# Softmax sums of a four-layer graph network on one core: layer 2's weights folded onto half the partitions and summed in one step of row and column tiles, layer 1's chunks summed on VectorE, biases added in pieces

## The chip, the cores and the metric

The kernel runs on one core of a Trainium2 chip. The core has a matrix engine (TensorE, PE in the profile, with its weight loads listed as PEld), three engines for elementwise work (VectorE is DVE, ScalarE is ACT, GpSimd is POOL), a queue engine (SyncE, SP) and 16 DMA engines. SBUF is the on-chip memory of 128 partitions; PSUM is where TensorE writes. Each engine works through its own instructions in order, and semaphores tie them together. The metric is the device time of one execution in microseconds. Before the change it was 2972.38 us, the median of 3 runs (2971.67 to 2974.36).

## The reference

32 graphs, each with 512 nodes of 256 features and a dense 512x512 adjacency matrix, go through four layers. Every layer adds its result to its input and normalises over the features.

```python
x = layernorm(x + gin(x, adj, eps, W1, b1, W2, b2))         # relu((1+eps)x + adj x) W1 ..., W2
x = layernorm(x + gat(x, adj, W, a_src, a_dst, bias))       # 4 heads, masked by adj > 0.5
x = layernorm(x + attention(x, adj, Wq, Wk, Wv, Wo, bo))    # 8 heads, scores + log(adj + 1e-6)
x = layernorm(x + masked_attention(x, nodemask, adj, W))    # 1 head, scores * adj
```

The code calls these layers 0 to 3. In layers 1 and 2 the attention weights of a head are exponentials e[j, i] of source node j and target node i. The output for target i is the sum over j of e[j, i] v[j], divided by the sum over j of e[j, i]. The change is about these divisors. All data are float32.

## The kernel before, in words

Weights of a head lie with the source nodes on the partitions: 512 sources are four chunks of 128 partitions, and each chunk has 512 targets along the free axis. So a divisor is a sum over chunks and over partitions, and TensorE makes the sum over partitions with a matrix of ones.

The work of each graph is cut into named steps. A step names an engine, an estimated time, the steps that it comes after, and the buffers that it takes and frees. Class `Plan` (line 47) walks over the steps of all graphs, with up to six graphs open at a time, and writes out the order of the instructions on every engine. It goes by due times and by a table of shifts per step name, which stands with a few other numbers in the last call, `plan.run`. The emitted order is then fixed: each engine does its instructions in that order and waits where data are late. Steps of graph g+1 and g+2 are thus mixed with those of graph g. Buffers come from counted stocks: 11 of 8 KB per partition ("B"), 12 of 4 KB ("C"), 17 of 2 KB ("D") and 8 PSUM banks ("p"). Step names carry numbers: h is a head, c a chunk, o a half of layer 2's heads, k = 4o + c.

The parts that the change and the prediction touch are these.

* Biases (`bias_steps`, L584): POOL adds one of three bias rows to the graph's x, 128 partitions by 1024 elements, in one instruction. x has to be ready before the layer's residual sum. These are the steps xb1, xb2 and xb3.
* Layer norm (`norm_steps`): VectorE takes statistics (L587, L588), adds epsilon to the variance (L604, on four elements), POOL raises it to the power -0.5 (L610, the rstd steps), VectorE makes a shift (L618), and ScalarE applies both (L628).
* Layer 0: transposes of the adjacency (L682), adj x (L715), the two products (L738, L757).
* Layer 1: ScalarE and VectorE make the weights of head h in buffer e{h}, four chunks of 512 (L909, L920; VectorE's steps are zm). The steps o1 (L943) multiply weights by values, two heads side by side as column tiles of 64, for chunks 0 and 1 and then for chunks 2 and 3. Steps ad{h}0 and ad{h}1 (L971) let an accumulating DMA, issued by POOL, add chunks 2 and 3 to chunks 0 and 1, and then chunk 1 to chunk 0. Step d1 (L991) sums the remaining chunk over partitions in column tiles of 32. The names aq and as that follow a DMA hold no instruction; they stand for its time on the queue and until landing.
* Layer 2: steps s{k} (L1113) make scores of chunk c for four heads at once, as four row tiles of 32; ScalarE takes exponentials (L1126, steps e), and VectorE multiplies with the adjacency (L1135, steps m, two heads each) into the buffer E{k} of 128 partitions by 4 heads by 512 targets. Steps n{k} (L1171) multiply weights by values, four heads side by side as column tiles of 32. Accumulating DMAs issued by POOL (`collect`, L1146, steps cd) add chunk 1 to chunk 0, chunk 3 to chunk 2, and then chunk 2 to chunk 0. One step d20 and one step d21 per graph (L1201) sum over the partitions: four column tiles of 32, each with a 128x32 matrix of ones, for four heads. ScalarE copies the result (L1213), VectorE takes the reciprocal (L1220, two halves) and multiplies (L1225), and the output projection follows (L1256). In the last graph no DMA collects the chunks, and d2 runs over all four chunks of each half.
* Layer 3: projections (L1300), scores (L1314), row maxima and exponentials, transposes (L1353), the product with x (L1368).

Of the kernel before, what the change touches and what calls it, by code (L numbers as in the profile page):

```python
# [14 lines left out]
ALU = mybir.AluOpType  # L15
AX = mybir.AxisListType

P = 128
# [209 lines left out]
def fast_path(  # L228
# [23 lines left out]
    nc = tc.nc  # L252
    B, N, D = x.shape
# [303 lines left out]
    def graph(g):  # L557
# [20 lines left out]
        def bias_steps(k, after):  # L578


            @step(f"xb{k}", "pool", 2.5, after + ("^bias",))
            def _():
                b = bias_bc[:, k - 1, None, :].to_broadcast([P, NC, D])
                nc.gpsimd.tensor_tensor(t["x"], t["x"], b, ALU.add)  # L584

        def norm_stats(n, c):
            nc.vector.bn_stats(t[f"st{n}"][:, c, :], t["xo" if n == 4 else "x"][:, c, :])  # L587
# [372 lines left out]
        plan.free("v1", ("o101", "o111"))  # L960

        for h in range(H1):
            after = (f"o1{h//2}0", f"zm{h}1")
            for k, m in enumerate((2, 1)):

                @step(f"ad{h}{k}", "pool", 0.95, after)
                def _(h=h, m=m):
                    z = t[f"e{h}"].rearrange("p c n -> p (c n)")  # L970
                    nc.gpsimd.dma_start(  # L971
                        z[:, : m * N], z[:, m * N : 2 * m * N], accum_op=ALU.add
                    )

                @step(f"aq{h}{k}", "qa", 1.5 * m, (f"ad{h}{k}",))
                def _():
                    pass

                @step(f"as{h}{k}", None, 2.5, (f"aq{h}{k}",))
                def _():  # L980
                    pass

                after = (f"as{h}{k}",)


        @step("d1", "pe", 0.95, tuple(f"as{h}1" for h in range(H1)), take=("p=d1",), mode="c32")
# [172 lines left out]
        def attend(k):  # L1159
# [26 lines left out]
                nc.scalar.copy(t["yT2"][:, o, :], t[f"n{o}"])  # L1186

            a = NC * o
            chunks = range(a, a + NC) if last else (a,)
            if not last:  # L1190
                collect(a + 2, a, (f"cs{a+1}", f"cs{a+3}", f"n{a+2}"))

            @step(
                f"d2{o}", "pe", 0.855 * len(chunks),
                tuple(f"m{b}1" for b in chunks) if last else (f"cs{a+2}",), take=(f"p=d2{o}",), mode="c32",
            )
            def _():
                t[f"d{o}"] = bank(f"d2{o}", [P, N], f"d2_ps_{o}")
                for b in chunks:
                    for j in range(4):  # L1200
                        nc.tensor.matmul(  # L1201
                            t[f"d{o}"][32 * j : 32 * j + 32, :], ones[:, :32], t[f"E{b}"][:, j, :],
                            start=(b == a), stop=(b == chunks[-1]),
                        )

            for b in chunks:
                for key in (f"E{b}", f"zs{b}"):
                    plan.free(key, (f"d2{o}", f"n{b}"))

            @step(f"nd{o}", "act", 0.49, (f"d2{o}",), take=(f"D=rdT{o}/1",), free=(f"d2{o}",))  # L1210
            def _():
                t[f"rd{o}"] = strip(f"rdT{o}", [P, N], f"rdT_{o}")
                nc.scalar.copy(t[f"rd{o}"], t[f"d{o}"])  # L1213
# [199 lines left out]
    for g in range(B):  # L1413
        graph(g)
    with tc.manual_schedule():
        plan.run([(28, 0.0, 6, 55.0, ((824592, 5.0), (893565, 10.0), (244737, 10.0), (23294, 5.0), (814168, 2.0), (264532, 2.0), (583369, 2.0), (708249, 5.0), (118144, 2.0), (603753, 2.0), (522046, 10.0), (973053, 5.0), (608632, 2.0), (603770, 2.0)), (0.5, 0.0, 0.0), (('Rl.q', 5.0), ('Rli', -10.5), ('Rs.q', -4.5), ('Rsi', 8.0), ('Rt', -14.5), ('ST', 4.5), ('ab', -6.0), ('ad00', -62.0), ('ad01', -61.5), ('ad10', -77.0), ('ad11', -51.5), ('ad20', -67.0), ('ad21', -32.5), ('ad30', -65.0), ('ad31', -48.0), ('aq00', 15.5), ('aq01', -16.0), ('aq10', 1.5), ('aq11', 2.5), ('aq20', -5.0), ('aq21', -5.0), ('aq30', 19.5), ('aq31', 61.0), ('at0', -1.5), ('at1', -36.0), ('at2', -12.0), ('at3', 8.5), ('atd0', 12.0), ('atd1', 5.0), ('atd2', -1.5), ('atd3', 6.5), ('ate0', 9.0), ('ate1', -57.5), ('ate2', 11.0), ('ate3', -0.5), ('cd1', -20.0), ('cd2', -16.5), ('cd3', -23.0), ('cd5', -10.0), ('cd7', -10.0), ('cq1', 6.0), ('cq2', -4.5), ('cq3', -55.5), ('cq6', -9.0), ('cq7', -15.0), ('d1', 4.5), ('d20', -2.5), ('d21', -4.5), ('de', -3.0), ('dev2.0', -11.0), ('dev4.0', -18.0), ('dt', -3.5), ('e00', -46.5), ('e02', -5.0), ('e03', 10.0), ('e10', -34.0), ('e12', -1.0), ('e13', -2.0), ('e20', -1.0), ('e21', -9.0), ('e22', -95.0), ('e23', -32.0), ('e30', -52.0), ('e31', -24.5), ('e32', -8.5), ('e33', 1.0), ('e42', -36.5), ('e43', -2.0), ('e50', -2.0), ('e51', -44.5), ('e53', -78.5), ('e60', -60.0), ('e61', -38.5), ('e62', -20.0), ('e63', -26.0), ('e70', -17.0), ('e71', -45.0), ('e72', -77.0), ('e73', -5.0), ('ed0', 46.5), ('ed1', 13.5), ('ed2', -19.5), ('ed3', 2.5), ('f0', 12.0), ('f1', 15.0), ('f3', -1.5), ('fe0', -12.0), ('fe1', -15.5), ('fe2', -8.0), ('fe3', 3.5), ('h0', -21.0), ('h1', -29.5), ('he0', -1.0), ('he1', 13.0), ('hsb.q', -1.0), ('hsbi', -2.0), ('hsl', -7.0), ('i0', 27.5), ('i1', 5.5), ('ie0', -1.0), ('ie1', 13.5), ('k0', -33.0), ('k1', 1.5), ('ke0', -10.0), ('ke1', 14.0), ('la0.q', 2.0), ('la0i', -32.0), ('la1.q', -32.5), ('la1i', -33.5), ('la2.q', -8.0), ('la2i', 20.0), ('la3.q', -3.0), ('la3i', 2.0), ('lb0.q', -44.0), ('lb0i', -35.0), ('lb1.q', 5.0), ('lb1i', -5.0), ('lb2.q', -33.0), ('lb2i', -37.0), ('lb3.q', -27.0), ('lb3i', -15.0), ('ldn.q', 3.0), ('ldni', -12.0), ('lx.q', 10.0), ('m00', -2.0), ('m01', 23.5), ('m10', 28.0), ('m20', 18.0), ('m21', -24.5), ('m30', 24.0), ('m31', 6.5), ('m40', 1.5), ('m41', -5.5), ('m50', 18.0), ('m51', -6.5), ('m60', 13.0), ('m61', 12.0), ('m70', 2.0), ('m71', 8.0), ('n0', 3.5), ('n1', 1.0), ('n2', -8.5), ('n4', 4.5), ('n5', -18.0), ('n6', -1.5), ('n7', 6.0), ('nd0', 16.0), ('nd1', -13.0), ('no0', 15.0), ('no1', 5.5), ('node', 11.5), ('o100', -38.5), ('o101', -4.5), ('o110', 3.0), ('o111', 5.5), ('oe0', 21.5), ('oe1', 78.5), ('out0.q', 7.0), ('out0i', 12.0), ('p0', 4.0), ('p1', -0.5), ('q0', 8.0), ('q1', 2.5), ('qe1', 2.0), ('r10', 1.0), ('r11', 15.0), ('r12', 81.5), ('r13', 10.0), ('r20', -12.5), ('r21', -15.5), ('r22', -4.0), ('r30', 2.0), ('r31', 46.0), ('r33', 4.5), ('r40', 42.5), ('r42', -15.5), ('r43', 4.5), ('rc00', 21.0), ('rc01', 0.5), ('rc10', 13.5), ('rd30', -10.0), ('rd32', 3.0), ('rd33', 2.0), ('s0', -1.5), ('s1', -36.0), ('s2', -2.0), ('s3', 0.5), ('s4', 14.0), ('s5', 3.5), ('s6', 6.5), ('s7', 8.5), ('sh1.0', 4.0), ('sh2.0', -31.5), ('sh3.0', 2.0), ('sh4.0', -3.0), ('st10', -1.0), ('st11', 13.5), ('st12', 24.5), ('st20', -7.5), ('st21', -8.0), ('st22', 7.0), ('st31', -3.0), ('st32', 3.0), ('st33', -8.5), ('st40', 6.0), ('st41', -6.5), ('st42', 6.5), ('st43', 20.5), ('t0', -7.0), ('t2', -8.5), ('t3', 0.5), ('ta0', -1.0), ('ta2', -3.0), ('ta3', -8.0), ('tb0', 4.0), ('tb1', 3.5), ('tb2', -10.5), ('tb3', 20.0), ('te1', -26.0), ('te2', -21.5), ('te3', 10.0), ('u0', 0.5), ('u1', -1.0), ('u2', -8.5), ('u3', -0.5), ('ue0', 1.5), ('ue1', 2.0), ('ue3', 22.0), ('v10', 8.0), ('v12', 10.0), ('v13', -1.5), ('v20', 1.0), ('v21', 1.5), ('v22', -14.5), ('v23', -35.5), ('va1.0', -19.0), ('va3.0', -0.5), ('ve10', 30.0), ('ve11', 10.0), ('ve12', 22.0), ('ve13', 31.5), ('ve20', 117.0), ('ve21', 58.0), ('ve22', 1.0), ('ve23', 6.5), ('w0', -2.0), ('w1', 2.0), ('w2', -17.0), ('w3', 5.5), ('wx0', -2.0), ('wx1', -1.0), ('wx2', -2.0), ('wx3', -15.5), ('x10', 4.5), ('x11', -10.0), ('x30', -22.0), ('x31', -13.0), ('xb1', -45.5), ('xb3', 2.0), ('xe10', 2.0), ('xe11', -61.5), ('xe20', -20.5), ('xe21', -8.5), ('xe30', 6.5), ('xe31', 3.5), ('xs.q', -1.5), ('xsi', 9.0), ('xt10', 9.5), ('xt20', 0.5), ('xt30', -2.0), ('xt31', -9.5), ('y0', 2.0), ('y1', -5.5), ('yd00', -21.0), ('yd01', 0.5), ('yd10', 10.5), ('yd11', -12.5), ('yn0', 7.5), ('yn1', 20.0), ('yn2', 26.0), ('yn3', 6.5), ('yt1', -3.0), ('yt2', -9.5), ('yt3', 5.5), ('z00', 9.5), ('z01', 4.5), ('z02', -18.0), ('z03', 51.0), ('z10', -2.0), ('z11', 3.0), ('z12', -1.0), ('z13', 31.0), ('z20', -2.0), ('z21', -21.0), ('z22', 45.0), ('z23', -4.0), ('z30', 40.0), ('z31', 3.0), ('z32', -27.5), ('z33', 10.0), ('zm00', -52.0), ('zm01', -4.5), ('zm10', -2.0), ('zm11', 7.0), ('zm20', -19.5), ('zm21', 7.5), ('zm30', -7.5), ('zm31', 2.0)))])

# [470 lines left out]
```

## Time and profile before

| what | value |
|---|---|
| median of 3 runs | 2972.38 us |
| time of the profiled execution | 2971.27 us |
| its span (first to last instruction) | 2969.4 us |
| mean granted TensorE clock | 0.997 |
| d2 (L1201) | 560 matmul records, 72.6 us busy |
| layer 1's DMA issues (L971) | 256, 512 KB and 256 KB by turns |
| layer 2's DMA issues (L1146) | 186 of 1024 KB |
| bias steps (L584) | 96, mean 2555 ns |
| software DMA queue | 295.73 MB, 51.4% of the 16 engines' span |
| all DMA | 448.93 MB, mean 151 GB/s |

How to read it: a row of a group of instructions has the line, engine and operation, written and read tiles with their shapes, the count, busy time and mean length of one in nanoseconds, and the idle time of the engine just before them with what ended it. A form such as 128*32 ahead of a shape is the part of TensorE's array that is used (rows by columns). A float32 matmul of two distinct data operands leaves two records. TensorE's matmuls are pipelined, so its busy share says that it always has something under way, not that it runs at its peak. The chain follows the work that ended last back from the end, at each step to what released it.

### The profile page before, as it was taken

The page shows a single profiled execution, that of the slowest core. Times are in us where ns is not written, and L with a number is a line of the kernel's source. Part 1 is how long each engine was busy: PE and PEld are TensorE (multiplying, and loading weights), DVE is VectorE, ACT ScalarE, POOL GpSimd, SP SyncE. Part 2 cuts the span into 40 slices and gives each one's busy share as a digit, 9 for nine tenths or more (in the row PEclk, how much of TensorE's full clock was granted, in tenths as well). Part 3 has the DMA queues.
Part 4 walks back from the last instruction along what each step waited for, and adds up shares of the span by engine and source line. Part 5 has one row for each costly group of instructions (what it writes and reads, how often), then busy time and mean ns, then how long its engine had stood idle before and what let it go on. Part 6 is the DMA issues. An engine that isn't in the chain of part 4 may idle for free.

```text
span 2969.4 us, 42791 instructions
## 1 busy us (share of the span) xinstructions
PE 2943.3 (99%) x15521; PEld 1668.0 (56%) x15521; DVE 2150.4 (72%) x4133; ACT 1927.3 (65%) x3818; POOL 801.4 (27%) x688
## 2 busy tenths in 40 slices
PE   8999999999999999999999999999999999999998
PEld 6545555555556555555555555555655555554545
DVE  3677777777777777677676777777777767767777
ACT  4666665667666676666676666766667666667664
POOL 1323222223232322222222222323232222223220
PEclk9999999999999999999999999999999999999999
DMA  4677766677766686666776666776668666677680
GB/s 146 137 156 174 165 153 140 145 158 169 166 146 140 140 183 162 154 134 143 176 165 155 137 148 156 170 166 146 139 140 185 159 156 133 142 176 157 138 178 16
DMA packets 153368, 448.93 MB, mean 151 GB/s; under 512 B 15232, under 2 KB 55360, under 8 KB 125248
## 3 DMA queue, kind: packets, MB, share of 16 engines
q0 software_dynamic: 63648, 295.73, 51.4%
q1 hardware_dynamic: 88112, 149.75, 15.4%
q8 instruction: 125, 2.05, 0.3%
q10 hardware_dynamic: 1392, 0.66, 0.1%
q14 instruction: 91, 0.75, 0.1%
HBM read 133.30 MB, written 17.07 MB: 51 GB/s over the span
## 4 chain that ended last, share of the span: by engine, by line
PE 85%; DVE 13%; DMA 1%; ACT 0%; issue 0%; POOL 0%; POOLq 0%; SPq 0%; ACTq 0%
PE h1T_ps L738 8%; PE s L1314 8%; PE hT_ps L715 8%; PE o_ps L1368 7%; PE y_ps L757 7%; PE o_ps L1171 6%; PE s L1113 6%; PE o_ps L943 5%; DVE z L1135 4%; PE v_ps L806 4%; PE v_ps L1094 4%; PE iT_ps L1300 4%; PE kT_ps L1076 4%; PE qT_ps L1076 4%; DVE st L587 2%; PE d_ps L1201 2%
## 5 line engine op out<-in xcount | busy, mean ns | idle before, releaser
L1126 ACT ACTIVATE z<-s 128x512 f32<-128x512 f32 x1024 | 551.3, 605 | 250.2 <-PE s L1113 250.0
L1135 DVE SCALAR_TENSOR_TENSOR z<-AT,z 128x1024 f32<-128x1024 f32 x512 | 625.6, 1241 | 95.7 <-ACT z L1126 93.0
L920 DVE SCALAR_TENSOR_TENSOR z<-z,T,edge 128x512 f32<-128x512 f32 x512 | 416.8, 857 | 38.2 <-ACT z L909 38.1
L1146 POOL DMA_DIRECT2D z<-z x186 | 164.1, 884 | 1005.5 <-DMA z<-z 358.7
L909 ACT ACTIVATE z<-R_bc,nT,S 128x512 f32<-128x512 f32 x512 | 376.6, 807 | 31.6 <-PE y_ps L757 22.4
L1220 DVE RECIPROCAL rdT<-rdT 128x256 f32<-128x256 f32 x128 | 215.9, 1725 | 188.3 <-ACT rdT L1213 188.3
L584 POOL TENSOR_TENSOR x<-x,bias_bc 128x1024 f32<-128x1024 f32 x96 | 245.2, 2555 | 395.0 <-PE xT_t L785 247.3
L971 POOL DMA_DIRECT2D z<-z x256 | 224.4, 970 | 457.0 <-DMA z<-z 168.4
L628 ACT ACTIVATE x<-x,shift,rstd 128x256 f32<-128x256 f32 x508 | 296.9, 600 | 52.1 <-DVE shift L618 51.5
L1171 PE MATMUL o_ps<-z,v 128*32 128x512 f32 x2048 | 295.3, 603 | 3.6 <-DVE z L1135 0.6
L1113 PE MATMUL s<-qT,kT 32*128 32x512 f32 x2048 | 288.1, 634 | 2.9 <-ACT qT L1082 2.9
L943 PE MATMUL o_ps<-z,v 128*64 128x512 f32 x1024 | 250.0, 609 | 2.7 <-DVE z L920 2.4
L738 PE MATMUL h1T_ps<-hT,w_sb 128*128 128x512 f32 x512 | 248.5, 610 | 0.0
L610 POOL TENSOR_TENSOR rstd<-ve,nhalf 128x4 f32<-128x4 f32 (+1 forms) x131 | 169.7, 1298 | 289.5 <-DVE ve L604 286.9
L1314 PE MATMUL s<-xT,iT 128*128 128x512 f32 x512 | 237.8, 599 | 0.0
L1368 PE MATMUL o_ps<-x,eT 128*128 128x256 f32 x1024 | 237.0, 379 | 0.1
L757 PE MATMUL y_ps<-w_sb,h1T 128*128 128x256 f32 x1024 | 230.8, 379 | 0.0
L757 PEld LDWEIGHTS y_ps<-w_sb,h1T 128*128 128x128 f32 x1024 | 194.2, 190 | 49.7 <-issue 25.8
L1368 PEld LDWEIGHTS o_ps<-x,eT 128*128 128x128 f32 x1024 | 193.8, 190 | 40.0 <-issue 13.6
L587 DVE BATCH_NORM_STATS2 st<-x 128x6 f32<-128x256 f32 x508 | 209.3, 412 | 4.7
L715 PE MATMUL hT_ps<-AT,x 128*128 128x384 f32 (+2 forms) x768 | 209.8, 382 | 0.0
L1113 PEld LDWEIGHTS s<-qT,kT 32*128 32x128 f32 x2048 | 87.2, 183 | 170.3 <-ACT z L1126 74.9
(152 smaller groups left out, 4236.8 us busy)
## 6 DMA issues: line engine op xcount, KB each, us to landing
z<-z POOLq DMA_DIRECT2D x186, 1024.0 KB, 8.7
A<-in_adj_dram SPq DMA_DIRECT2D x256, 256.0 KB
z<-z POOLq DMA_DIRECT2D x128, 512.0 KB, 5.5
R_bc<-R_dram SPq DMA_DIRECT2D x32, 1024.0 KB
z<-z POOLq DMA_DIRECT2D x128, 256.0 KB, 3.8
x<-in_x_dram SPq DMA_DIRECT2D x32, 512.0 KB
out_dram<-x SPq DMA_DIRECT2D x31, 512.0 KB
nm<-in_nodemask_dram SPq DMA_DIRECT2D x32, 256.0 KB
```

The lines of the kernel that those rows point to most:

```text
L715: nc.tensor.matmul(ph[:, cols], t["x"][:, m, blk(d)], moving, start=(k == 0), stop=(k == len(parts) - 1),)
L738: nc.tensor.matmul(ph, w1_sb[:, d, blk(f)], t["hT"][:, d, :], start=(d == 0), stop=(d == DC - 1))
L757: nc.tensor.matmul(py[:, j, :], t["h1T"][:, f, blk(2 * c2 + j)], w2_sb[:, f, :], start=(f == 0), stop=(f == HC - 1),)
L909: nc.scalar.activation(t[f"e{h}"][:, c, :], t["Rbc"][:, h, :], AF.Relu, bias=t["nT"][:, h, c : c + 1], scale=t["S"][:, h, c : c + 1],)
L920: nc.vector.scalar_tensor_tensor(z, z, t["T"][:, h, c : c + 1], t["edge"][:, c, :], op0=ALU.add, op1=ALU.mult)
L943: nc.tensor.matmul(po[j * F1 : (j + 1) * F1, :], t["v"][:, c, h * F1 : (h + 1) * F1], t[f"e{h}"][:, c, :], start=(c == 0), stop=(c == NC - 1),
L1113: nc.tensor.matmul(pk, t["k"][hs, o, blk(c)], t["q"][hs, o, :], start=True, stop=True)
L1126: nc.scalar.activation(t[f"E{k}"][:, j, :], t[f"ps{k}{j}"], AF.Exp, scale=QSCALE)
L1135: nc.vector.scalar_tensor_tensor(z, t["AT"][:, c, None, :].to_broadcast([P, 2, N]), ADJ_EPS, z, op0=ALU.add, op1=ALU.mult,)
L1171: nc.tensor.matmul(t[f"n{o}"][32 * j : 32 * j + 32, :], t["v2"][:, c, o * P + F2 * j : o * P + F2 * (j + 1)], t[f"E{k}"][:, j, :], start=( ...
L1314: nc.tensor.matmul(pt, t["iT"][:, d, blk(c)], t["xT3"][:, d, :], start=(d == 0), stop=(d == DC - 1),)
L1368: nc.tensor.matmul(py, t[f"eT{c}"][:, blk(m)], t["x"][:, m, :], start=(m == 0), stop=(m == NC - 1),)
```

## The change

There are three edits, and the planner's numbers differ.

1. In layer 2, behind the collecting DMAs, a further accumulating DMA per half (steps fd0 and fd1, issued by POOL) adds 64 partitions of the summed weights to the other 64: partitions 64 to 127 are added to 0 to 63 for the first four heads, and 0 to 63 to 64 to 127 for the last four. One step d2 per graph then sums both halves: eight matmuls, each on a tile of 64 rows by 32 columns, the first half's on the lower rows and the second half's on the upper rows, into two PSUM banks. The last graph keeps its form.
2. In layer 1, VectorE adds the chunks in place (128x1024, then 128x512 per head) where DMAs did.
3. A bias is added in four instructions of 128x256.

```diff
-            @step(f"xb{k}", "pool", 2.5, after + ("^bias",))
+            @step(f"xb{k}", "pool", 2.7, after + ("^bias",))
             def _():
-                b = bias_bc[:, k - 1, None, :].to_broadcast([P, NC, D])
-                nc.gpsimd.tensor_tensor(t["x"], t["x"], b, ALU.add)
+
+                for c in range(NC):
+                    nc.gpsimd.tensor_tensor(
+                        t["x"][:, c, :], t["x"][:, c, :], bias_bc[:, k - 1, :], ALU.add
+                    )
...
         for h in range(H1):
             after = (f"o1{h//2}0", f"zm{h}1")
             for k, m in enumerate((2, 1)):

-                @step(f"ad{h}{k}", "pool", 0.95, after)
+                @step(f"as{h}{k}", "dve", (1.08, 0.55)[k], after)
                 def _(h=h, m=m):
-                    z = t[f"e{h}"].rearrange("p c n -> p (c n)")
-                    nc.gpsimd.dma_start(
-                        z[:, : m * N], z[:, m * N : 2 * m * N], accum_op=ALU.add
-                    )
-
-                @step(f"aq{h}{k}", "qa", 1.5 * m, (f"ad{h}{k}",))
...
-                @step(f"as{h}{k}", None, 2.5, (f"aq{h}{k}",))
...
-                after = (f"as{h}{k}",)
+                    z = t[f"e{h}"]
+                    nc.vector.tensor_add(z[:, :m, :], z[:, :m, :], z[:, m : 2 * m, :])
+
+                after = (f"as{h}0",)
...
             a = NC * o
-            chunks = range(a, a + NC) if last else (a,)
             if not last:
                 collect(a + 2, a, (f"cs{a+1}", f"cs{a+3}", f"n{a+2}"))
+                low, high = slice(0, P // 2), slice(P // 2, P)
...
+                @step(f"fd{o}", "pool", 0.95, (f"cs{a+2}", f"n{a}"))
+                def _():
+                    z = t[f"E{a}"].rearrange("p h n -> p (h n)")
+                    src, dst = (low, high) if o else (high, low)
+                    nc.gpsimd.dma_start(z[dst], z[src], accum_op=ALU.add)
+
+                @step(f"fq{o}", "qa", 3.0, (f"fd{o}",))
...
+                @step(f"fs{o}", None, 2.5, (f"fq{o}",))
...
+                if o == 0:
+                    return
+
+                @step("d2", "pe", 0.95, ("fs0", "fs1"), take=("p=d20", "p=d21"), mode="c32")
+                def _():
+                    for q in range(2):
+                        t[f"d{q}"] = bank(f"d2{q}", [P, N], f"d2_ps_{q}")
+                    for j in range(4):
+                        for q, part in enumerate((low, high)):
+                            nc.tensor.matmul(
+                                t[f"d{q}"][32 * j : 32 * j + 32, :], ones[part, :32],
+                                t[f"E{NC*q}"][part, j, :], start=True, stop=True,
+                            )
+
+                for q in range(2):
+                    for key in (f"E{NC*q}", f"zs{NC*q}"):
+                        plan.free(key, ("d2", f"n{NC*q}"))
+                for q in range(2):
+                    normalise(q, "d2")
+                return
+
+            chunks = range(a, a + NC)
...
-        plan.run([(28, 0.0, 6, 55.0, ((824592, 5.0), (893565, 10.0), (244737, 10.0),
...
+        plan.run([(24, 0.1, 6, 100.0, ((959604, 5.0), (114893, 5.0), (536715, 2.0),
...
```

`normalise` is the former tail of this function (copy, reciprocals, products), now called once for each half behind d2. In the planner's last call the period goes from 28 to 24, the look-ahead from 0.0 to 0.1, the weight of a change of tiling from 55 to 100, and the seeds and shifts are others, so that the order of nearly all steps changes on every engine.

## The prediction, made before the changed kernel was run

> **What bounds the kernel now.** I read the page first (busy shares, then the chain that ended last), then the chain in order of time over one graph, then the timelines where that chain leaves TensorE.
>
> ```profile
> PE 2943.3 (99%) x15521; PEld 1668.0 (56%) x15521; DVE 2150.4 (72%) x4133; ACT 1927.3 (65%) x3818; POOL 801.4 (27%) x688
> ...
> PE 85%; DVE 13%; DMA 1%; ACT 0%; issue 0%; POOL 0%; POOLq 0%; SPq 0%; ACTq 0%
> ```
>
> TensorE is busy throughout and holds 85% of the chain. No DMA or POOL row holds it, so what is removed from TensorE's stream counts in full, and what is removed elsewhere counts only where TensorE waits. From the chain in order of time (start, length, what):
>
> ```profile
> 1061.31 1.72 PE h1T_ps L738 x4
> 1063.03 1.07 PE s L1113 x8
> 1064.10 1.85 PE o_ps L1171 x16
> 1065.95 1.07 PE s L1113 x8
> 1067.02 1.91 PE h1T_ps L738 x4
> ...
> 1069.81 1.00 PE o_ps L1171 x8
> 1070.81 0.86 PE d_ps L1201 x8
> ```
>
> One float32 matmul leaves two records. Two full ones (L738 x4) take 1.72, so 0.86 each; a step of four column tiles (d_ps L1201 x8, four matmuls) takes the same 0.86 behind another of its shape. Where the tiling changes, the step that enters pays: full tiles 1.91-1.72 = 0.2, row tiles (s L1113) 1.07-0.86 = 0.21, column tiles of 32 (o_ps L1171) 0.14. The same chain shows o_ps L943, columns of 64, at 1.87 against 1.72: 0.15. The period of a graph in the middle of the run is 91.3 us (start of iT_ps L1300 to that of the next graph).
>
> The 13% on DVE is one stretch per graph, 1028.1 to 1041.6, and it ends in a real wait:
>
> ```profile
> 1033.46 2.03 DVE L604 TENSOR_SCALAR ve<-mv 128x4 f32<-128x4 f32 x1
> ...
> 1036.54 0.15 DVE L604 TENSOR_SCALAR ve<-mv 128x4 f32<-128x4 f32 x1
> ```
> ```profile
> 1033.11 2.36 POOL L584 TENSOR_TENSOR x<-x,bias_bc 128x1024 f32<-128x1024 f32 x1 [9.33 <-PE xT_t L785]
> ```
> ```profile
> 1040.49 2.20 PE L1171 MATMUL o_ps<-z,v 128*32 128x512 f32 x8
> 1042.62 0.71 PE L806 MATMUL v_ps<-wg_sb,xT 128*128 128x264 f32 x2
> ```
> ```profile
> PEld o_ps L1171 <- DVE z L1135: 33.2, 40, 1.3
> ```
>
> An instruction on four elements took 2.03 us instead of 0.15: it ended (1035.49) when POOL's whole bias step ended (1035.47). Behind it DVE is late with the weights of one attend step: its first two heads start at 1040.49, the other two wait until 1041.63, and the step holds TensorE for 2.13 us instead of 1.00. That is 1.13 us; the waits view has 33.2 us of it, some 30 graphs.
>
> **The change, part by part.**
>
> *d2.* Two steps of 0.86 per graph become one of eight tiles (64 rows by 32 columns), in 31 graphs; the last graph keeps its four-chunk form. The row: four row tiles (L1113) and four column tiles (L1171) each run at four times one matmul, so eight should take one pass length, 0.86, saving 31 x 0.86 = 26.7. Against this speaks the Trainium skill, "TensorE: Matmul & The Clock Gate", Part 3, packing small matmuls: a 3x3 packing in rows and columns measured 6.32x of 9, 0.70 of the ideal. By that share eight tiles give 5.6x, the step costs 8 x 0.86/5.6 = 1.23 and only 31 x 0.49 = 15 is saved. I take the row: the page also gives 3.07x for four row tiles, where this trace shows 4.0x in a stream. Bounds: 0 saved (two fours in turn) to 26.7.
>
> *Changes of tiling.* The new order on TensorE, read from the built programs, enters a new tiling 844 times instead of 851: full -32, row +27, 64 columns -33, the new 64x32 +31, others equal. -32 x 0.2 + 27 x 0.21 - 33 x 0.15 + 31 x 0.17 = -0.4 (0.17 lies between 0.14 and 0.21; no row shows this shape). In the middle of the run 26 entries per graph become 25. I count -1 in all.
>
> *The bias in pieces.* Four adds of 128x256 replace one of 128x1024 (2555 ns mean on L584). At a quarter each they take 0.64 and the step stays near 2.6; if each carries a fixed cost, 1 us is my upper estimate, 4 us a step. POOL is 27% busy and holds none of the chain, so either is hidden. What matters: a DVE instruction can be held for a piece, 0.64, not for 2.4. Also, in the new order, the delayed attend step stands about 2 us behind its weights by the sums below. I take the 1.13 us wait as gone: 30 x 1.13 = 34. Bounds: 0 to 34.
>
> *Layer 1's sums on DVE.* Out go 256 accumulating DMAs (128 of 512 KB, 128 of 256 KB) with 224 us of POOL issue; 128 adds of 128x1024 and 128 of 128x512 come in.
>
> ```profile
> L1135 DVE SCALAR_TENSOR_TENSOR z<-AT,z 128x1024 f32<-128x1024 f32 x512 | 625.6, 1241 | 95.7 <-ACT z L1126 93.0
> L1330 DVE TENSOR_TENSOR z<-s,A 128x512 f32<-128x512 f32 x128 | 87.3, 682 | 9.4 <-PE s L1314 9.4
> L971 POOL DMA_DIRECT2D z<-z x256 | 224.4, 970 | 457.0 <-DMA z<-z 168.4
> ```
>
> Start to start in the chain these are 1.13 and 0.60, so 128 x 1.73 = 221 us: DVE goes from 2150 to 2371, 81% of the new time. Hidden as long as DVE's in-order queue keeps ahead of TensorE. The tight place is d1: in the new order the first half of the second-issued o1 pair (heads 0 and 1) ends 5.6 us of TensorE work ahead of d1, and six adds stand between: 3 x 1.13 + 3 x 0.60 = 5.2, with 0.4 for the two handovers. By mean durations 3 x 1.24 + 3 x 0.68 = 5.8. So d1 waits 0 to 0.6 us; I take 0.3, 32 x 0.3 = +9. Queued behind the adds on DVE are the next attend weights (L1135, L1127 in the changed kernel) and the reciprocals; each has over 5 us before its reader on TensorE. I laid DVE's queue over one period of TensorE's order with these durations and found some 8 us idle ahead of the y steps, so a lag does not pile up.
>
> *The fold.* Two DMAs of 64 partitions by 8 KB (512 KB) per graph, issued by POOL (62 x 0.88 us), each waiting for the collects; behind them on POOL stand the rstd steps that DVE's shift needs. Landing from the DMA rows:
>
> ```profile
> z<-z POOLq DMA_DIRECT2D x186, 1024.0 KB, 8.7
> ...
> z<-z POOLq DMA_DIRECT2D x128, 512.0 KB, 5.5
> ```
>
> By size, 5.5. The skill's "SBUF — State Buffer", Door 1, speaks against it: partition bit 6 picks the port half, so a destination of 64 partitions reaches half the ports; by that the fold lands like 1024 KB, 8.7. Needed from the last score step to d2: about 8 (scores, exponentials, weights, issues) + 8.7 + 8.7 + 5.5 = 31, or 34 by the page. The new order has about 55 us of TensorE work there (39 before). Hidden both ways; if that cover were gone, each us late would cost 31. The rstd that d1's neighbourhood needs stands behind the second fold with some 15 us to spare. The sum of the first four heads now holds its buffer (one of eleven) for some 81 us from its last score step to d2 (31 before), and the four reciprocals of a graph (1.73 each) come due together; d2 to the output projection is 28 us of TensorE work (11 before), against some 11 for copies, reciprocals and products. DMA load falls: 295.7 MB on the software queue, minus 100.7, plus 32.5.
>
> *Sum*, against the profiled execution (2971.3, of which 2969.4 is span): -26.7 - 1 - 34 + 9 = -53, giving 2918.6. The median of the runs shown is 1.1 above the profiled execution: about 2919.
>
> **Rivals.**
>
> *The wait moves (0.18).* DVE carries 10% more and some attend or o1 step waits about 1.1 us per graph as before. For: DVE at 81%. Against: the slack above. -26.7 - 1 + 9 gives 2953.
>
> *Eight tiles run as two fours (0.06).* For: no row shows both tilings at once. -1 - 34 + 9 gives 2946.
>
> *d1 behind DVE (0.08, slower).* One mechanism: the add chain ahead of d1 starts late, because the adds before it wait for o1, or because GpSimd's pieces hold them. All gain (62 us) is gone at 62/32 = 1.9 us of wait per graph; at 3 us it is 2972.4 - 62 + 96 = 3006. Against: my count gives 0 to 0.6.
>
> *More (0.05):* no wait at d1 and a tighter start-up (the first 200 us idle TensorE some 14 us): 2898.
>
> *Unchanged (0.03)*: losses that happen to cancel.
>
> **How the numbers follow.** The likeliest case has 0.60, its own range 2909 to 2940 (d1 at 0 to 0.6 us, the eight tiles at 0.86 to 1.23). Eight in ten must reach into the two middling rivals: 2900 to 2958 leaves out d1 behind DVE, the unchanged case and a tail. Measurements of this kernel tell 0.2% (6 us) from no change. Faster: 0.60 + 0.18 + 0.06 + 0.05 = 0.89; same 0.03; slower 0.08.
>
> **What would show it.** Right: a period near 89.6 us; the 64-row d_ps group with half of TensorE's time per graph; o_ps waiting for DVE's weights (L1127 there) near zero; no instruction of L604's kind (L607 there) over about 0.8 us; d1's wait for the adds under 0.6. Wrong: d1 waiting over 1 us, d_ps records starting in two batches, d2 waiting for a DMA, or the attend step still split.

## Result, and the profile after

The changed kernel takes 2950.6 us (median of 4 runs, 2948.3 to 2953.9) where the kernel before takes 2972.0 (median of 4): a ratio of 0.9928, 95% interval 0.9911 to 0.9945. It is faster by 21 us, 0.7%; the forecast was 53. The lines of code have moved: L604 is L607 now, L1113 is L1105, L1171 is L1163, L1201 is L1210, L715 is L718, L664 is L667.

The page of the changed kernel (busy shares, the chain's shares by engine, one group, one row of DMA issues):

```profile
PE 2890.2 (98%) x15521; PEld 1651.0 (56%) x15521; DVE 2344.2 (80%) x4389; ACT 1906.5 (65%) x3818; POOL 704.4 (24%) x782
...
PE 76%; DVE 14%; DMA 7%; ACT 2%; issue 1%; POOL 0%; POOLq 0%; SPq 0%; ACTq 0%; DVEq 0%
...
L585 POOL TENSOR_TENSOR x<-x,bias_bc 128x256 f32<-128x256 f32 x384 | 343.9, 994 | 211.4 <-PE xT_t L788 156.3
...
z<-z POOLq DMA_DIRECT2D x62, 512.0 KB, 6.0
```

TensorE lost 53 us of busy time (2943.3 before), as much as the whole forecast, but the time fell by 21 only. DMA has 7% of the chain, 1% before. The fold lands 6.0 us after its issue: near the 5.5 that the forecast took by size, and not the 8.7 that it had for half the ports. The attend steps' wait for VectorE's weights, 33.2 us in 40 waits before, is down to 5.5 in 8, and d1 waits once for VectorE's sums (waiting engine and line, what it waited for: us in total, times, longest):

```profile
PEld o_ps L1163 <- DVE z L1127: 5.5, 8, 1.1
...
PE d_ps L983 <- DVE z L973: 1.2, 1, 1.2
```

In the chain in order of time, d2 is one pass (start, length, what; the length runs to the next step's start):

```profile
1090.44 1.02 PE d_ps L1210 x16
1091.46 1.07 PE s L1105 x8
```

In the same trace an attend step of four full-height column tiles (L1163) that stands between two score steps takes 1.00, and d2 with its eight tiles 1.02. The eight start within 0.05 us of each other (1090.37 to 1090.42), again 0.45 us later for the second record of each, and the next step follows. So eight tiles of 64x32 do run at once.

Where the gain went is in two waits views of the changed kernel, TensorE's and that of the queue SP:

```profile
PE hT_ps L718 <- DMA x<-in_x_dram: 17.7, 16, 2.3
PE hT_ps L718 <- ACT x L631: 11.4, 9, 1.9
...
SPq L667 <- PE v_ps L809: 418.3, 26, 28.8
```

and in the timeline of one graph (start, length; what ended a wait in brackets):

```profile
1030.04 0.86 POOL L1138 DMA_DIRECT2D z<-z  x1 [5.13 <-DVE z L1127]
1031.27 0.82 POOL L1191 DMA_DIRECT2D z<-z  x1 [0.37 <-DMA z<-z]
...
1033.56 0.38 SPq L667 DMA_DIRECT2D x<-in_x_dram  x1
...
1037.76 4.48 PE L1401 MATMUL o_ps<-x,eT 128*128 128x256 f32 x20
1043.15 0.46 PE L718 MATMUL hT_ps<-ATd,x 128*128 128x128 f32 x2 [0.92 <-ACT x L631]
```

The aggregation h (L718) reads x of its graph. In the new order the queue SP issues that load (L667) only after layer 1's value step (L809) of another graph has given back a 4 KB buffer. By the packets in the trace the load's first packet moves 4.0 to 4.7 us after issue and its last ends at 8.7 to 10.4; h starts some 0.6 us later. Just ahead of it POOL has issued a collect (L1138) and a fold (L1191). Before the change the load was issued 80 us ahead of h and took 3.3 to 4.2 us. From the timeline of the kernel before:

```profile
970.07 0.40 SPq L664 DMA_DIRECT2D x<-in_x_dram  x1
...
1049.88 0.49 PE L715 MATMUL hT_ps<-ATd,x 128*128 128x128 f32 x2
```

The wait is 1.36 us on average in the 24 graphs of the middle (0.7 to 2.5), 32.6 us in all: summed from TensorE's starts, less each step's own length. The period of a graph is 89.9 to 91.5 us, 91.31 before.

### The profile page after: what moved, and what is told of

Same layout as the page of the kernel before. It is cut to its first block, busy times and chain, and to the rows that moved or that the text cites. A ratio compares the mean times of both kernels' runs of the same rounds, so it can differ in the third digit from the quotient of the medians.

```text
span 2946.9 us, 42883 instructions
## 1 busy us (share of the span) xinstructions
PE 2890.2 (98%) x15521; PEld 1651.0 (56%) x15521; DVE 2344.2 (80%) x4389; ACT 1906.5 (65%) x3818; POOL 704.4 (24%) x782
## 4 chain that ended last, share of the span: by engine, by line
PE 76%; DVE 14%; DMA 7%; ACT 2%; issue 1%; POOL 0%; POOLq 0%; SPq 0%; ACTq 0%; DVEq 0%
PE s L1347 8%; PE hT_ps L718 7%; PE o_ps L946 7%; PE h1T_ps L741 7%; PE y_ps L760 7%; PE s L1105 6%; DMA x<-in_x_dram 5%; PE o_ps L1163 5%; DVE z L1127 4%; PE iT_ps L1333 4%; PE v_ps L1086 3%; PE qT_ps L1068 3%; PE kT_ps L1068 3%; PE o2p_ps L1289 2%; PE xT_t L1049 2%; PE AT_t L685 2%
## 5 line engine op out<-in xcount | busy, mean ns | idle before, releaser
L912 ACT ACTIVATE z<-R_bc,nT,S 128x512 f32<-128x512 f32 x512 | 390.3, 817 | 164.7 <-PE y_ps L760 138.1
L1138 POOL DMA_DIRECT2D z<-z x186 | 166.6, 898 | 1147.2 <-PE s L1105 329.1
L923 DVE SCALAR_TENSOR_TENSOR z<-z,T,edge 128x512 f32<-128x512 f32 x512 | 401.6, 829 | 45.4 <-ACT z L912 45.2
L585 POOL TENSOR_TENSOR x<-x,bias_bc 128x256 f32<-128x256 f32 x384 | 343.9, 994 | 211.4 <-PE xT_t L788 156.3
L631 ACT ACTIVATE x<-x,shift,rstd 128x256 f32<-128x256 f32 x508 | 285.1, 607 | 136.5 <-DVE shift L621 136.0
L613 POOL TENSOR_TENSOR rstd<-ve,nhalf 128x4 f32<-128x4 f32 (+1 forms) x131 | 147.7, 1128 | 806.7 <-DVE ve L607 792.9
L1105 PE MATMUL s<-qT,kT 32*128 32x512 f32 x2048 | 293.2, 639 | 4.1 <-ACT qT L1074 4.1
L1163 PE MATMUL o_ps<-z,v 128*32 128x512 f32 x2048 | 257.8, 600 | 0.2 <-DVE z L1127 0.2
L973 DVE TENSOR_TENSOR z<-z 128x1024 f32<-128x1024 f32 (+1 forms) x256 | 230.7, 953 | 2.0 <-PE o_ps L946 1.9
L741 PE MATMUL h1T_ps<-hT,w_sb 128*128 128x512 f32 x512 | 231.4, 593 | 0.0
L718 PE MATMUL hT_ps<-AT,x 128*128 128x384 f32 (+2 forms) x768 | 209.8, 382 | 0.1
L1377 ACT ACTIVATE z<-z,nmax 128x512 f32<-128x512 f32 x128 | 92.4, 722 | 132.4 <-DVE nmax L1369 131.4
```

Of the source, the lines that this page charges most:

```text
L718: nc.tensor.matmul(ph[:, cols], t["x"][:, m, blk(d)], moving, start=(k == 0), stop=(k == len(parts) - 1),)
L741: nc.tensor.matmul(ph, w1_sb[:, d, blk(f)], t["hT"][:, d, :], start=(d == 0), stop=(d == DC - 1))
L912: nc.scalar.activation(t[f"e{h}"][:, c, :], t["Rbc"][:, h, :], AF.Relu, bias=t["nT"][:, h, c : c + 1], scale=t["S"][:, h, c : c + 1],)
L923: nc.vector.scalar_tensor_tensor(z, z, t["T"][:, h, c : c + 1], t["edge"][:, c, :], op0=ALU.add, op1=ALU.mult)
L1105: nc.tensor.matmul(pk, t["k"][hs, o, blk(c)], t["q"][hs, o, :], start=True, stop=True)
L1163: nc.tensor.matmul(t[f"n{o}"][32 * j : 32 * j + 32, :], t["v2"][:, c, o * P + F2 * j : o * P + F2 * (j + 1)], t[f"E{k}"][:, j, :], start=( ...
```

## The experiments

The kernel before ran beside each of the four groups of experiments (medians of 2971.8 to 2972.6 us). Times are medians of 4 runs, of 7 for after_bias_whole. The period is that of the middle graphs, from one iT step to that of the next graph.

| kernel | us | ratio to before, 95% | period, us |
|---|---|---|---|
| x_early | 2916.1 | 0.9812 [0.9796, 0.9829] | 88.97 |
| x_late | 2952.1 | 0.9938 [0.9921, 0.9955] | 89.8 to 93.3 |
| after_no_fold | 2911.2 | 0.9798 [0.9782, 0.9814] | 88.97 |
| x_early_no_fold | 2911.6 | 0.9798 [0.9782, 0.9814] | 88.97 |
| x_early_unfolded | 2932.7 | 0.9868 [0.9851, 0.9884] | 89.67 |
| x_early_tail | 2921.3 | 0.9831 [0.9814, 0.9847] | 88.97 |
| x_early_bias_whole | 2952.5 | 0.9936 [0.9919, 0.9952] | 90.23 |
| after_bias_whole | 2980.0 | 1.0029 [1.0017, 1.0040] | 90.9 to 94.1 |
| x_early_no_bias | 2906.3 | 0.9778 [0.9762, 0.9794] | 88.97 |
| before_bias_pieces | 2987.9 | 1.0053 [1.0036, 1.0069] | 91.5 to 92.7 |
| before_no_bias | 2934.8 | 0.9874 [0.9858, 0.9891] | 90.16 |
| x_early_no_sums | 2906.7 | 0.9782 [0.9766, 0.9799] | 88.96 |

### Is it the late load of x?

**x_early.** The order stays; the buffers are handed out again, one more of them, the one free longest first.

```diff
+        for kind, n in (("C", 13), ("D", 16)):
+            self.respread(kind, n, order)
...
+            for k, key, _ in s.take:
+                if k == kind:
+                    self.slot[g][key] = room.pop(0)
...
+                if not left[g][k] and self.kind[g][key] == kind:
+                    room.append(self.slot[g][key])
```

> The changed kernel with the order on every engine unchanged; only the 4 KB buffers are handed out anew over 13 instead of 12 (the strips of 2 KB over 16 instead of 17 to make room), so that the load of x takes a buffer that the y transposes gave back some 9 us before layer 1's value step gives one back. Theory A, the late load: the load is issued some 18 us ahead of its reader instead of 8 to 9, the 1.36 us wait ahead of the aggregation (24 graphs, 32.6 us) goes, and the time falls from 2950.6 to about 2918, period near 89.2. Theory B, the wait belongs to something else that ends just then (ScalarE's normalisation of the graph before, or the clearing of a PSUM bank), the load only ends beside it: the time stays at 2945 to 2951. Theory C, the load lands late because the queue is shared with collects, whenever it is issued: part of the gain only, 2930 to 2945.

Measured: 2916.1, 34.5 us below the changed kernel, theory A. The timeline of x_early:

```profile
1014.26 0.87 POOL L1156 DMA_DIRECT2D z<-z  x1
...
1014.62 0.38 SPq L685 DMA_DIRECT2D x<-in_x_dram  x1
...
1027.12 5.35 PE L1419 MATMUL o_ps<-x,eT 128*128 128x256 f32 x24
1032.31 0.38 PE L736 MATMUL hT_ps<-ATd,x 128*128 128x128 f32 x2
```

The load goes out 17.7 us ahead of h. Issued 0.4 us behind a collect (L1156), it still takes 8.7 to 10.1 us to land, but now nobody waits: no idle time stands ahead of h, and of the two rows of h in the waits view one wait of 0.4 us is left. The row that put part of the wait down to ScalarE (L631) named what ended last there, not the cause: the order is the same here, and h does not wait.

**x_late.** The same thirteen buffers, x on the one given back last.

```diff
-                    self.slot[g][key] = room.pop(0)
+                    self.slot[g][key] = room.pop(int(key == "x" and g > 5))
```

> As x_early, thirteen buffers and the same order on every engine, but from the seventh graph on the load of x takes the buffer that layer 1's value step gives back last, as in the changed kernel (the strips go over 15 instead of 16, since the buffers come out a little larger). Theory A, only the moment of the load counts: the wait ahead of the aggregation is back and the time returns to about 2950. Rival, the thirteenth buffer helped in other places: it stays near 2916.

Measured: 2952.1. The thirteenth buffer alone is worth nothing; the moment of the load is worth the 34 to 36 us.

**after_no_fold.** The load as late as in the changed kernel, without what POOL issued just ahead of it.

```diff
-                    nc.gpsimd.dma_start(z[dst], z[src], accum_op=ALU.add)
+                    pass
```

> The changed kernel, the load of x as late as there, without the 62 fold DMAs (layer 2's denominators lack half their terms). Is it the fold issued just ahead of the load that makes it land 8.7 to 10.4 us after its issue? If so it lands some 4 us earlier, the wait ahead of the aggregation goes, and the time is near 2915. If the load takes that long beside whatever else moves there, the wait stays, and the time is 2951 less the 4.5 us that the folds cost in the early version: about 2946.

Measured: 2911.2. The timeline of after_no_fold:

```profile
1020.64 0.86 POOL L1138 DMA_DIRECT2D z<-z  x1 [5.14 <-DVE z L1127]
...
1024.16 0.38 SPq L667 DMA_DIRECT2D x<-in_x_dram  x1
...
1027.49 5.35 PE L1401 MATMUL o_ps<-x,eT 128*128 128x256 f32 x24
1032.67 0.38 PE L718 MATMUL hT_ps<-ATd,x 128*128 128x128 f32 x2
```

The load is issued 8.5 us ahead of h, as late as the order has it, but its last packet now ends 5.4 to 6.8 us after issue, and h does not wait. So two things together make the wait: the order issues the load with 8.5 us to spare, and the fold in front of it makes it land some 3.5 us later. Removing either removes all of it.

### What are d2 and the fold worth?

**x_early_unfolded.** No fold, and full-height columns in two passes.

```diff
-                    for j in range(4):
-                        for q, part in enumerate((low, high)):
+                    for q in range(2):
+                        for j in range(4):
                             nc.tensor.matmul(
-                                t[f"d{q}"][32 * j : 32 * j + 32, :], ones[part, :32],
-                                t[f"E{NC*q}"][part, j, :], start=True, stop=True,
+                                t[f"d{q}"][32 * j : 32 * j + 32, :], ones[:, :32],
+                                t[f"E{NC*q}"][:, j, :], start=True, stop=True,
                             )
```

> As x_early, and layer 2's weights are not folded: no fold DMA, and the one step d2 holds two sums of four full-height column tiles (eight matmuls of 128 rows in turn) instead of eight half-height tiles at once. The result is the same. Against x_early: if eight half-height tiles cost one pass, 0.86 us more in 31 graphs, +26.7 us; by the share that the Trainium skill gives for a packing in rows and columns (TensorE: Matmul & The Clock Gate, Part 3), 0.49 us, +15; if the folds on the queue cost something elsewhere, less than that.

Measured: +16.6 against x_early. That looks like the estimate from the page of the Trainium skill (+15), but the two kernels differ in the folds too.

**x_early_no_fold.** Only the folds are left out (the edit of after_no_fold on x_early).

> As x_early without the 62 fold DMAs; d2 stays at eight half-height tiles, so layer 2's denominators lack half their terms. If the folds lie beside other work, as forecast, the time stays within 3 us of 2916; if they cost by the queue, by POOL's issue or by a wait of d2, it falls by 5 to 10, and then that much of the 16.6 us between x_early and x_early_unfolded was theirs.

Measured: 2911.6, so the folds cost 4.5 us even where x is early. The period is the same; from one iT step to the next, two stretches near the end are 2.6 and 2.7 us shorter. Against this kernel x_early_unfolded is 21.1 us slower, and that is the price of d2 alone. In the middle graphs it can be read: d2 follows d1, which also uses columns of 32. With eight half-height tiles the way from d1's last start to d2 and on to the scores is 0.20 + 1.02 us, with two full-height passes 0.08 + 1.84. The difference is 0.70, and 31 x 0.70 = 21.7. The pass saved is 0.86; 0.16 is lost again where the tiling changes, 0.12 of it between d1 and d2 (0.20 for 0.08). The estimate that the forecast made from the Trainium skill ("TensorE: Matmul & The Clock Gate", Part 3, 6.32x for nine tiles) was 0.49 saved, before any change of tiling.

**x_early_tail.** The last three graphs without folds (the very last has none anyway), d2 there in two passes.

```diff
+                    if g < B - 3:
                         nc.gpsimd.dma_start(z[dst], z[src], accum_op=ALU.add)
...
+                    for q in range(2 if g >= B - 3 else 0):
+                        for j in range(4):
+                            nc.tensor.matmul(
+                                t[f"d{q}"][32 * j : 32 * j + 32, :], ones[:, :32],
+                                t[f"E{NC*q}"][:, j, :], start=True, stop=True,
+                            )
```

> As x_early, the last three graphs without a fold: their d2 sums full-height columns in two passes, so the result is the same. The folds cost 4.5 us, and between the starts of the i steps of the last graphs two stretches are 2.6 and 2.7 us shorter without them, so they should cost only there. If so: 2916 less 4.5 plus 3 x 0.7 for the second pass, about 2914 to 2912; if the folds cost in all graphs, no gain.

Measured: 2921.3, 5 us slower than x_early, a miss. The two stretches keep their length (101.35 and 84.60 us, 101.32 and 84.63 in x_early), so the folds that cost there belong to earlier graphs. The profiled execution is 5.6 us longer than that of x_early, and laid beside it, 0.9 us stand at an attend step in the first 200 us, 1.7 are the second passes (2 x 0.83), and 3.0 come behind the last matmul, where the program ends: there POOL's closing semaphores follow those of SP after 3.3 us, in x_early at once. Why they do is not shown; those 3.0 us stand behind all work on the graphs.

What the folds cost near the end can be read by laying x_early beside x_early_no_fold: most of the lost time stands ahead of matmuls of one y step (1.9 us) and one o1 step (2.5). Both stand behind ScalarE's work on layer 1 (L930), and that waits for another load, R_bc, of 1024 KB. The first of the two places, in x_early and then in x_early_no_fold:

```profile
2537.48 1.15 POOL L1209 DMA_DIRECT2D z<-z  x1
...
2543.38 0.34 SPq L882 DMA_DIRECT2D R_bc<-R_dram  x1
...
2556.38 0.81 ACT L930 ACTIVATE z<-R_bc,nT,S 128x512 f32<-128x512 f32 x1 [5.94 <-DMA R_bc<-R_dram]
```

```profile
2544.56 0.34 SPq L882 DMA_DIRECT2D R_bc<-R_dram  x1
...
2554.24 0.81 ACT L930 ACTIVATE z<-R_bc,nT,S 128x512 f32<-128x512 f32 x1 [2.67 <-DMA R_bc<-R_dram]
```

From the load's issue to ScalarE's start it is 13.0 us with the folds and 9.7 without, at the second place 12.3 and 9.0. So the folds again make a load that stands behind them later, by 3.3 us. This is read from two traces; no run moves that load alone.

### What does the bias do?

**before_no_bias.** The kernel before without its bias steps.

> The kernel before, order unchanged, without the GpSimd bias step (the three biases are left out of the result). If the hold of VectorE by that step is what makes an attend step 1.13 us late in 30 graphs, the wait goes: about 2938. If VectorE is late there by its own work, and the hold only adds to it, less: 2945 to 2965. If the hold has no part in it, 2972.

Measured: 2934.8, 37.2 us less. Laid beside the kernel before, TensorE's starts differ in one attend step, by 1.15 us per graph. So the bias step causes that wait. The run alone does not part the hold of VectorE from a POOL that is busy; the trace of the kernel before does: POOL's next instruction, rstd, starts at 1036.78, 1.3 us after the bias step's end, when VectorE's late `ve` of 1036.54 is there.

**before_bias_pieces.** The kernel before with four instructions per bias.

> The kernel before, its order unchanged, with the bias in four GpSimd instructions of 128x256. If the one long instruction alone made the wait of 1.13 us in 30 graphs, it goes and the time falls from 2972 to about 2938 (-34). If VectorE is late there for another reason too, or four pieces of about 0.9 us hold it one after another, less: -10 to -25. If the wait is paid somewhere else, no change.

Measured: 16 us slower than before. None of the three answers that I wrote down allowed a loss. Its timeline, around the attend step shown before:

```profile
1036.23 4.10 POOL L584 TENSOR_TENSOR x<-x,bias_bc 128x256 f32<-128x256 f32 x4 [8.90 <-PE xT_t L787]
1040.30 3.00 POOL L612 TENSOR_TENSOR rstd<-ve,nhalf 128x4 f32<-128x4 f32 x2
...
1037.00 0.68 DVE L606 TENSOR_SCALAR ve<-mv 128x4 f32<-128x4 f32 x1
1037.59 1.21 DVE L1137 SCALAR_TENSOR_TENSOR z<-AT,z 128x1024 f32<-128x1024 f32 x1
1038.73 0.69 DVE L606 TENSOR_SCALAR ve<-mv 128x4 f32<-128x4 f32 x1
...
1039.67 1.75 DVE L1137 SCALAR_TENSOR_TENSOR z<-AT,z 128x1024 f32<-128x1024 f32 x1
...
1042.35 0.16 DVE L620 SCALAR_TENSOR_TENSOR shift<-mv,rstd 128x4 f32<-128x4 f32 x1 [0.59 <-POOL rstd L612]
...
1045.59 1.05 PE L1173 MATMUL o_ps<-z,v 128*32 128x512 f32 x4 [0.51 <-DVE z L1137]
```

One hold of 1.9 us (2.03 for 0.15) has become three of about 0.53 (0.68 for 0.15, twice, and 1.75 for 1.21), 1.6 in sum. The four pieces take 4.1 us on POOL instead of 2.36, so the rstd steps behind them are later and VectorE's shift waits 0.59 for them. The attend step is 1.56 us late instead of 1.15, and another one 22 us later loses up to 0.4 more.

**after_bias_whole**, and **x_early_bias_whole** on a kernel without the wait for x. In both the four adds become one again.

```diff
-                for c in range(NC):
-                    nc.gpsimd.tensor_tensor(
-                        t["x"][:, c, :], t["x"][:, c, :], bias_bc[:, k - 1, :], ALU.add
-                    )
+                b = bias_bc[:, k - 1, None, :].to_broadcast([P, NC, D])
+                nc.gpsimd.tensor_tensor(t["x"], t["x"], b, ALU.add)
```

> The changed kernel with the order unchanged and the bias again in one GpSimd instruction. If the pieces removed the hold on VectorE, it comes back: a small VectorE instruction near 2 us, and either the wait of 1.1 us per graph (30 graphs, +34 us, about 2985), or, if the new order alone had taken the attend step out of reach, no change in time (within 3 us of 2950.6) with the long VectorE instruction in the trace all the same.

> As x_early with the bias again in one GpSimd instruction. The price of the pieces where TensorE has no other wait: if the 29 us that the whole bias cost on the changed kernel were its own, about 2945; if they were partly the wait for x in another place, 2920 to 2935; if the new order had made the pieces needless, 2916.

Measured: +29.3 against the changed kernel, and +36.4 against x_early. In the new order the pieces are worth what I had forecast for them. But the wait that comes back is another one. The timeline of x_early_bias_whole:

```profile
1204.09 2.37 POOL L603 TENSOR_TENSOR x<-x,bias_bc 128x1024 f32<-128x1024 f32 x1 [6.37 <-PE d_t L1016]
...
1204.28 2.47 DVE L1274 TENSOR_TENSOR yT<-yT,rdT 128x256 f32<-128x256 f32 x1
1206.67 0.74 DVE L1034 TENSOR_TENSOR y<-y_t,rd 128x256 f32<-128x256 f32 x2
...
1205.85 2.40 PE L1121 MATMUL s<-qT,kT 32*128 32x512 f32 x8
...
1207.13 0.29 PEld L1121 LDWEIGHTS s<-qT,kT 32*128 32x128 f32 x2 [0.98 <-DVE y L1034]
```

and that of x_early at the same place:

```profile
1188.83 3.43 POOL L603 TENSOR_TENSOR x<-x,bias_bc 128x256 f32<-128x256 f32 x4 [5.98 <-PE xT_t L806]
...
1189.41 0.43 DVE L1276 TENSOR_TENSOR yT<-yT,rdT 128x256 f32<-128x256 f32 x1
1189.76 0.74 DVE L1036 TENSOR_TENSOR y<-y_t,rd 128x256 f32<-128x256 f32 x2
...
1190.98 1.14 PE L1123 MATMUL s<-qT,kT 32*128 32x512 f32 x8
```

A product of 0.43 us takes 2.47 and ends 0.3 us after the bias instruction. Behind it VectorE reads two PSUM tiles (L1034) late, a score step waits for their banks, and it spreads over 2.40 us instead of 1.14. Laid beside x_early, TensorE is 1.26 us later from that step on, in every graph. With pieces the two reads come in time. The attend steps, the victims before, wait for their weights 6.7 us in the whole run of x_early_bias_whole and 5.5 in that of x_early (33.2 in the kernel before).

**x_early_no_bias.** No bias steps on x_early.

> As x_early without the GpSimd bias steps (the three biases are left out of the result). What do the four pieces still cost, where one instruction cost 36 us more? If nothing on TensorE waits for what they hold, 2914 to 2916, and the period stays at 88.97; if a part of the hold is left in each graph, the period falls and the time with it, to 2905 or less; if only the start and the last graphs feel them, 2908 to 2913 at an unchanged period.

Measured: 9.8 us less, at the same period; 6.5 of them in the two stretches near the end that the folds lengthen as well, 2.3 in the first 210 us. So the pieces are not free there.

### What do layer 1's sums on VectorE cost?

**x_early_no_sums.**

```diff
-    nc.gpsimd.memset(tiny_n, TINY * N)
+    nc.gpsimd.memset(tiny_n, 1.0)
...
-                    z = t[f"e{h}"]
-                    nc.vector.tensor_add(z[:, :m, :], z[:, :m, :], z[:, m : 2 * m, :])
+                    pass
```

> As x_early without layer 1's 256 adds on VectorE (the denominators hold one chunk of four, with 1 added so that they stay finite). What do the 221 us more on VectorE cost? By the trace, d1 waits for them once (1.4 us): 2914 to 2916. By the forecast's term, 0.3 us in each of 32 graphs: 2907. If VectorE at 80% also delays the start and the last graphs: 2900 to 2910.

Measured: 9.4 us less, near the forecast's term, yet not where it had it. The period stays (88.96): in x_early d1 waits for the sums once in the whole run (1.2 us). 5.4 of the 9.4 are again in the two stretches near the end, 3.6 in the first 210 us. Folds, sums and bias pieces each cost something in the same few graphs, so 4.5, 9.4 and 9.8 must not be added.

## Why the prediction was wrong, point by point

The step that failed is the fold, which the sum has at nothing: "Hidden both ways; if that cover were gone, each us late would cost 31." I priced it by its own reader, d2, and d2 never waits for it. I did not ask whose transfer it stands in front of. The load of x is that transfer: h waits 24 times, 1.36 us on average, and without the wait x_early is 34.5 us faster. The sentence that should have led there, "DMA load falls", was an average: fewer bytes in all, but a new 512 KB in the 3 us ahead of one load. The other half of the cause was readable as well. I had laid out VectorE's queue in the new order, but not SP's, where the issue of x had moved from 80 us ahead of its reader to 8.5.

The rest of the sum stands better. Without this one wait the time is x_early's 2916.1, against a forecast of 2919. That the two are so close is in part luck: as the points below show, d2 gave 6 us less than the forecast had, the new order some 11 more, and the folds and the bias pieces cost 4.5 and 9.8 us, overlapping, that the sum did not have.

* **d2**, -26.7 with all changes of tiling at -1: it is -21.1 (x_early_unfolded to x_early_no_fold). Eight tiles in one pass held, against the 0.70 of the ideal that I had worked out from the page's 6.32x of 9; what I missed is that d1 had left the columns of 32 set, so the new shape pays 0.16 more. The new order gains more than -1 elsewhere: between before_no_bias (90.16) and x_early_unfolded (89.67), which have the same matmuls and no stalls in the middle graphs, lie 0.49 us a graph, 24 x 0.49 = 12 us.
* **The hold**, -34: removing it is worth -37.2 in the old order. That "a DVE instruction can be held for a piece, 0.64, not for 2.4" held in both orders, but my step from there to "I take the 1.13 us wait as gone" did not: in the old order pieces lose 16 us. In the new one the attend step had left the place, and another reader took it. A piece took 0.99 us on average: my upper estimate, not a quarter of the whole.
* **d1**, +9: right in size (9.4) by luck, for it is wrong in place. d1 waits once in the whole run and not in each graph; the price is paid in the first and the last graphs.
* **Rivals.** "The wait moves" gave 2953, 2 us from what was measured, and a wait did come in the old one's place. But the number is luck: the rival named VectorE and an attend or o1 step, and it was SP's load and h. I gave it 0.18 and argued against it with VectorE's slack alone. The eight tiles as two fours, and d1 behind VectorE, are ruled out by the trace.
* **Signs.** The period was to be near 89.6; x_early has 88.97, the changed kernel 89.9 to 91.5. The 64-row group takes 34.0 us in 31 graphs where d2 took 72.6 in all 32 (7.3 of it now in the last), half per graph; the o_ps wait is 5.5 us in all, L607 0.701 at most, and d1 waits once, 1.2 us: but for that one wait these signs were met. My list of what would show it wrong had d2 waiting for a DMA, and no other load.

The version to keep is x_early: 2916.1 us, 1.9% below the kernel before, with the changed kernel's work and order.

## What to carry to other kernels

When an order changes, read for every load the time from its issue to its reader, and set it against how long it takes to land beside what is issued just ahead; a new transfer is priced by whom it delays, not only by who reads it. An instruction that another engine holds is a property of the place: cut the holder into pieces only after looking what is held, and what stands behind the holder, in that very order. A sum can have nearly every term right and still miss, if it lists only the waits that the old trace shows.

## What the runs showed of the hardware that I had not expected

* A GpSimd add of 128x1024 takes 2.37 us in the stretches shown; the same in four instructions takes 3.43 in one order and 4.10 in another. In these stretches some VectorE instructions that start beside it end with it or 0.3 us later, 2.03 us for 0.15 and 2.47 for 0.43; beside pieces they take about 0.5 us more than alone. Others beside it, statistics and a reciprocal among them, keep their lengths; what decides between them, the runs don't show.
* The 512 KB load of x lands 3.3 to 4.2 us after its issue where the kernel before has it, 5.4 to 6.8 some 3.5 us behind the issue of a 1024 KB collect, and 8.7 to 10.4 with a fold of 512 KB between the two. A fold is not needed for that: at its place in x_early, 0.4 us behind a collect, the load takes 8.7 to 10.1, and at the same place in x_early_no_fold, which has no fold at all, 8.6 to 11.4.
* Eight float32 matmuls on tiles of 64 rows by 32 columns take one pass: 1.02 us to the start of the row tiles behind them, where four full-height ones of an attend step take 1.00, and eight full-height ones, in two passes, 1.84.
